# The 5x5 depthwise convolution of layer 0, taken over 16 image lines at once

## The chip, the core and the metric

The kernel runs on one core of one Trainium2 chip. A core has five engines that run beside each other and wait for one another through semaphores: TensorE (PE, matrix products), VectorE (DVE), ScalarE (ACT), GpSimd (POOL) and SyncE (SP, which here issues the transfers). The metric is the device time of one execution in microseconds (us), the median of several runs.

## The reference

Two layers run one after the other on 16 images of 128 channels and 56 x 56 pixels, in fp32. Layer 0, which the change touches, is a routed window attention:

```python
x = x + dwconv3x3(x, pos_w, pos_b)                    # per channel
y = layernorm(x) ; q, k, v = split(y @ qkv_w + qkv_b)
# 7 x 7 windows of 8 x 8 pixels; each window attends to the 4 windows
# whose mean key fits its mean query best; 4 heads of 32 channels
o = attention(q, gathered k, gathered v)
lepe = dwconv5x5(v, lepe_w, lepe_b)                   # per channel, 25 taps
x = x + (o + lepe) @ wo_w + wo_b
x = x + gelu(layernorm(x) @ mlp_w1 + mlp_b1) @ mlp_w2 + mlp_b2
```

Layer 1 (a 3x3 convolution, a small state-space recurrence over 8 tokens per pixel, a group norm) follows and is not touched.

## The kernel before

All of layer 0 is written out in one program order, and each engine keeps that order (`_chain`). Channels lie on the 128 partitions. An image is 7 blocks of 8 lines, 448 columns each (`BLK`), and a block holds 7 windows. The images go through a software pipeline: while image `im` attends, the next image `nxt` is normalised and projected, and the one after it (`far`) begins its 3x3 convolution on POOL.

**Steps.** `step(im, nxt, t)` runs once for each of the 49 windows; r = t // 7 is the window row and c = t % 7 the place in it. A step does `scores` (PE, into the PSUM tile `ps`, of which there is one), `largest` (DVE, L415), `exponentials` (ACT, L421), `inverse` (DVE reciprocal, L427), `weights` (POOL, L431), and for earlier windows the transposes (L453, L439), their copies (ACT, L459, L446) and `attend` (PE, L469). Over the seven steps of a row it also carries two layer norms and the projections: at c = 1 the sum of attention and convolution (`collect`, L516) and the output projection (L524), at c = 2 the residual (L528) and the centring product (L319), at c = 3 the square and variance product (L323, L327), at c = 4 the deviation (ACT, L331, L332), `second` (DVE, L532) and the next image's centring, at c = 5 its variance, at c = 6 its deviation and `windows` (DVE, L340, L348). POOL does the 3x3 taps of the next image (`beside`, L313, L315) spread over t = 0 to 44.

**The convolution.** `surround(im, r)` (POOL, L484) lays the 8 lines of block r with 2 lines above and below into one of three padded tiles `vpads` of 12 lines. `convolve` (DVE, L506 for the first tap, L512 for the others) multiplies one tap's shifted view by its weight and adds it to a sum in PSUM; the 25th tap writes `lepe` in SBUF. Two sums are kept in two banks (`sums_`). `convolve_on(n)` makes the next n taps of the schedule. Consecutive places in the schedule belong to two different blocks, whose sums lie in different banks:

```python
r = at // 25
r -= (r - at) % 2
convolve(images[r // NBLK], r % NBLK, (at - 25 * r) // 2)
```

A row of steps makes 4, 2, 2, 3, 3, 3, 2 taps (`TAPS`), all but one of a step's taps ahead of the reciprocal and one at the end of the step.

**MLP.** After the 49 steps, `mlp(im, nxt)` takes 7 blocks (6 for the first image) in turns m = 0, 1, ...: `expand` (PE and ACT, L542, L543), then for the block before it `contract` (PE, L548), whose last part is the DVE sum `r` (L550) and its transfer to DRAM (SP, L551). `r` comes from a pool of three buffers (`w3`). Turn m = 0 makes 10 taps, turns 1 to 5 make 7, 7, 6, 6, 6. At m = 2 SP issues the 20 gathers for the first five windows of the next image (L396), ahead of that turn's transfer of `r`. At m = 1 and 2 POOL makes 30 operations of `beside` for `far`; before that, at m = 0, it runs `surround(nxt, 2)`. In the turn before the last the scores of the next image's window 0 are begun (`open_step`), and its reciprocal follows in step 0.

Of the kernel before, what the change touches and what calls it, by code (L numbers as in the profile page):

```python
# [10 lines left out]
F32 = mybir.dt.float32  # L11
U32 = mybir.dt.uint32
AF = mybir.ActivationFunctionType
ALU = mybir.AluOpType
# [3 lines left out]
P = 128  # L18
H = W = 56
HW = H * W  # L20
WIN = 7
NW = WIN * WIN
WP = 64
BLK = 448
# [184 lines left out]
def layer0(ctx: ExitStack, tc: tile.TileContext, x, t, x1, conv):  # L209
# [42 lines left out]
    def bank(name):  # L252
        return banks.tile([P, 512], F32, tag=name, name=name)

    g0, ptt, pvt, po, *sums_ = (bank(k) for k in ("g0", "ptt", "pvt", "po", "lepe0", "lepe1"))
    ps = banks.tile([P, 2, 512], F32, tag="ps", name="ps")
# [19 lines left out]

    vpads = [cst.tile([P, 12, W + 4], F32, tag=f"vpad{k}", name=f"vpad{k}") for k in range(3)]
    for v in vpads:
# [38 lines left out]
    def centred(at, im, i):  # L317
        held["pc"] = at[:, 0:BLK]
        nc.tensor.matmul(held["pc"], lhsT=centre, rhs=im["xh"][i], start=True, stop=True)  # L319
# [155 lines left out]

    def vpad(im, r):
        return vpads[(im["b"] * NBLK + r) % 3]

    def surround(im, r):

        v = vpad(im, r)

        def put(lines, i, rows):
            nc.gpsimd.tensor_copy(  # L484
                v[:, lines, 2 : W + 2].rearrange("c r (w x) -> c w r x", x=8),
                im["kv"][:, WIN * i : WIN * i + WIN, :, 1].rearrange("c w (r x) -> c w r x", x=8)[:, :, rows, :],
            )

        put(slice(2, 10), r, slice(0, 8))
        if r == 0:  # L490
            nc.gpsimd.memset(v[:, 0:2, :], 0.0)
        else:
            put(slice(0, 2), r - 1, slice(6, 8))
        if r == NBLK - 1:
            nc.gpsimd.memset(v[:, 10:12, :], 0.0)
        else:
            put(slice(10, 12), r + 1, slice(0, 2))

    def convolve(im, r, k):

        v = vpad(im, r)
        acc = sums_[(im["b"] * NBLK + r) % 2][:, 0:BLK].rearrange("c (h w) -> c h w", w=W)
        dy, dx = divmod(k, 5)
        src = v[:, dy : dy + 8, dx : dx + W]
        if k == 0:
            nc.vector.tensor_scalar(acc, src, lep[:, 0:1], lepe_b, ALU.mult, ALU.add)  # L506
            return
        out = acc
        if k == 24:
            lepe = im["lepe", r] = w2.tile([P, BLK], F32, tag="lepe", name=f"lepe_{im['b']}_{r}")  # L510
            out = lepe.rearrange("c (h w) -> c h w", w=W)
        nc.vector.scalar_tensor_tensor(out, src, lep[:, k : k + 1], acc, ALU.mult, ALU.add)  # L512

# [31 lines left out]
    def contract(im, i, k):  # L545
        pm = (g0, po)[k % 2][:, 0:BLK]
        for s in range(3):
            nc.tensor.matmul(pm, lhsT=wm2[:, s, :], rhs=im["hid", i][:, s, :], start=(s == 0), stop=(s == 2))  # L548
        r = w3.tile([P, BLK], F32, tag="r", name=f"r_{im['b']}_{i}")
        nc.vector.scalar_tensor_tensor(r, pm, mlp_b2, im["xh"][i], ALU.add, ALU.add)  # L550
        nc.sync.dma_start(x1[im["b"]][:, i * BLK : (i + 1) * BLK], r)  # L551

    TAPS = (4, 2, 2, 3, 3, 3, 2)

    slot = [0]

    def convolve_on(count):


        for at in range(slot[0], slot[0] + count):
            r = at // 25
            r -= (r - at) % 2
            if 0 <= r < NB * NBLK:
                convolve(images[r // NBLK], r % NBLK, (at - 25 * r) // 2)
        slot[0] += count

# [4 lines left out]
    def step(im, nxt, t):  # L573
# [32 lines left out]
        if c == 6 and new:  # L606
            windows(nxt, r)
        convolve_on(TAPS[c] - 1)
        if new:
# [8 lines left out]
        inverse(im, t)  # L618
        if t in (1, 8, 17, 27):
            surround(im, 3 + (1, 8, 17, 27).index(t))  # L620
        if t in (36, 44) and new:
            surround(nxt, (t - 36) // 8)
        weights(im, t)
# [8 lines left out]
        if c % 2 == 0:  # L632
            transpose_values(im, t)
            keep_values(im, t)
        convolve_on(1)
        if waits:
# [31 lines left out]
    def mlp(im, nxt):  # L668
# [9 lines left out]
        for m in range(count + 1):  # L678
# [10 lines left out]
            if m == 0:  # L689
                transpose_weights(im, NW - 1)  # L690
                keep_weights(im, NW - 1)
                if nxt:
                    for s in (1, 2):
                        project(g0, s)
                        keep(nxt, last, s)
                convolve_on(10)
                if nxt:
                    surround(nxt, 2)
                elif early:
                    first(last, range(5, 9))  # L700
# [7 lines left out]
            if m > 0:  # L708
                contract(*blocks[m - 1], m)
            if 1 <= m <= 5:  # L710
                convolve_on((7, 7, 6, 6, 6)[m - 1])
            if far and m in (1, 2):
# [13 lines left out]
    def norm_begun(i):  # L726

        centred((g0, sums_[1])[i % 2], im, i)
        means[i] = held["pc"]
        squared(f"0_{i}")  # L730
# [8 lines left out]
    for i in range(NBLK):  # L739
# [12 lines left out]
        if i >= NBLK - 3:  # L752
            convolve_on(8)
        held["pc"] = means[i]
        windows(im, i)
        for s, at in enumerate((pvt, po, ps[:, 0, :])):
            project(at, s)
            keep(im, i, s)
# [7 lines left out]
    surround(im, 2)  # L766
    convolve_on(32)
    if NB > 1:
# [548 lines left out]
```

## Time and profile before

| what | value |
|---|---|
| median of 3 runs | 8326.0 us (8321.87 to 8326.96) |
| the profiled execution | 8321.03 us, of which the profile's span is 8319.0 us |
| layer 0 | from 0 to about 3154 us of the span |
| from one image to the next | 1406.3 to 1594.0 us at the same instruction (L382): 187.7 us |
| busy in 1500 to 2000 us | PE 463.6, DVE 457.2, POOL 410.7, ACT 363.9 of 500 us |
| one tap, 128 x 448 (L512) | 2688 in all, 677 ns each |

Times in the views are counted from the start of the span. A line of the timeline gives the start, the time from the first start to the last end, the engine, the source line, the operation, how many of it, and in brackets the idle time of the engine before it with what ended that. A line of the windows gives a stretch, its length, then the busy time of PE, PE's weight loads, DVE, ACT and POOL with the number of instructions in brackets, the granted clock of PE, the share of the DMA engines and GB/s.

### The profile page before, as it was taken

The numbers are of one execution on the slowest core, as the hardware profiler recorded it, in microseconds if no ns is written. First come the engines' busy times: TensorE is split into PE (matmuls) and PEld (weight loads), VectorE is DVE, ScalarE is ACT, GpSimd is POOL, SyncE is SP. The second block draws the span as 40 slices with busy tenths as digits, with TensorE's granted clock in tenths as the row PEclk, the third lists the DMA queues.
The fourth block names the chain that finished last, engine by engine and source line by source line (L and its number), as shares of the span: only waits on it lengthen the run. The fifth ranks groups of instructions, "written<-read, shape, count | busy, mean of one in ns | idle before, by whom it ended". The sixth has DMA issues, their size and how long they took to land.

```text
span 8319.0 us, 151598 instructions
## 1 busy us (share of the span) xinstructions
PE 7858.1 (94%) x52860; PEld 3316.4 (40%) x52860; DVE 7746.6 (93%) x10342; ACT 5659.3 (68%) x10598; POOL 7064.8 (85%) x5696
## 2 busy tenths in 40 slices
PE   5999999999999998999999999999999999999997
PEld 3444444444444453333333333333333333333332
DVE  7999999999999976999999999999999999999997
ACT  4777777777777755666666666666666666666665
POOL 7888888888888725899999989999999999999987
PEclk8999999999999998999999999999999999999998
DMA  3333333333333332334333333334334334333333
GB/s 65 86 87 88 85 89 88 87 87 87 88 86 87 79 85 80 87 89 105 98 92 99 101 92 98 96 92 104 95 93 108 86 98 108 84 101 102 89 93 80
DMA packets 764424, 757.86 MB, mean 91 GB/s; under 512 B 188688, under 2 KB 663952, under 8 KB 761616
## 3 DMA queue, kind: packets, MB, share of 16 engines
q1 hardware_dynamic: 763664, 748.18, 34.9%
q8 instruction: 422, 6.91, 0.4%
q14 instruction: 338, 2.77, 0.1%
HBM read 439.61 MB, written 102.76 MB: 65 GB/s over the span
## 4 chain that ended last, share of the span: by engine, by line
DVE 39%; POOL 25%; PE 18%; issue 10%; ACT 7%; DMA 1%; SPq 0%; POOLq 0%; ACTq 0%; DVEq 0%
DVE h L991 11%; DVE a L1001 10%; DVE h L1002 6%; POOL cst L1006 5%; POOL xh L315 5%; POOL e L431 4%; PE a L973 4%; POOL tap L313 3%; DVE lepe L512 3%; PE x L984 2%; POOL dtx L925 2%; DVE sst L415 2%; PE pq L1015 2%; DVE ud L960 2%; PE pq L184 1%
## 5 line engine op out<-in xcount | busy, mean ns | idle before, releaser
L1006 POOL TENSOR_TENSOR cst<-h,cb 128x1792 f32<-128x1792 f32 x784 | 3129.8, 3999 | 375.4 <-DVE h L1002 301.2
L976 ACT ACTIVATE a<-a 128x896 f32<-128x896 f32 x1568 | 1415.8, 903 | 1119.7 <-PE x L984 678.6
L991 DVE TENSOR_TENSOR h<-x,bb 128x896 f32<-128x896 f32 x1568 | 1696.0, 1082 | 91.0 <-PE x L984 51.2
L512 DVE SCALAR_TENSOR_TENSOR lepe<-vpad,lep,lepe 128x448 f32<-128x448 f32 x2688 | 1717.0, 677 | 0.5
L973 PE MATMUL a<-dt,adec 32*128 32x448 f32 x6272 | 1613.0, 590 | 35.6 <-DVE h L1002 16.2
L984 PE MATMUL x<-dtx,amask 32*128 32x448 f32 x6272 | 1616.1, 591 | 32.2 <-DVE h L991 24.5
L1002 DVE TENSOR_TENSOR h<-a,h 128x896 f32<-128x896 f32 x1344 | 1466.8, 1091 | 45.8
L1001 DVE TENSOR_TENSOR a<-a,h 128x896 f32<-128x896 f32 x1344 | 1463.7, 1089 | 3.7 <-ACT a L976 3.7
L431 POOL TENSOR_SCALAR e<-e,sst,zero 128x256 f32<-128x256 f32 x1568 | 861.1, 560 | 466.2 <-DVE sst L427 417.6
L421 ACT ACTIVATE e<-ps,sst 128x256 f32<-128x256 f32 x1568 | 728.6, 469 | 521.6 <-DVE sst L415 471.0
L315 POOL TENSOR_TENSOR xh<-xh,tap 128x448 f32<-128x448 f32 x749 | 859.4, 1147 | 43.7
L973 PEld LDWEIGHTS a<-dt,adec 32*128 32x128 f32 x6272 | 472.2, 184 | 1050.9 <-DVE h L1002 474.0
L184 PE MATMUL pq<-pad,conv 128*128 128x448 f32 x1890 | 834.7, 559 | 0.0
L1015 PE MATMUL pq<-cst,sel 128*32 128x448 f32 x6272 | 730.2, 550 | 1.0 <-POOL cst L1006 1.0
L415 DVE TENSOR_REDUCE sst<-ps 128x2 f32<-128x512 f32 x784 | 539.8, 688 | 107.4 <-PE ps L409 83.6
L146 ACT ACT_TABLE_LOAD x491 | 630.0, 1283 | 9.2 <-PEq L1308 0.7
L984 PEld LDWEIGHTS x<-dtx,amask 32*128 32x128 f32 x6272 | 473.1, 184 | 400.1 <-DVE h L991 378.7
L453 PE MATMUL ptt<-ident,e 128*128 128x128 f32 x3136 | 538.4, 283 | 97.0 <-POOL e L431 80.3
L409 PE MATMUL ps<-sel,q 32*64 32x256 f32 x6272 | 537.2, 411 | 51.8 <-ACT e L421 45.6
L313 POOL TENSOR_SCALAR tap<-pad,pos,zero 128x448 f32<-128x448 f32 x749 | 548.7, 733 | 35.7
L453 PEld LDWEIGHTS ptt<-ident,e 128*128 128x128 f32 x3136 | 366.6, 141 | 420.4 <-POOL e L431 240.8
L459 ACT COPY att<-ptt 128x512 f32<-128x512 f32 x784 | 458.6, 585 | 73.7 <-PE ptt L453 65.8
(173 smaller groups left out, 12025.5 us busy)
## 6 DMA issues: line engine op xcount, KB each, us to landing
sel<-kv SPq DMA_DIRECT2D x3136, 64.0 KB
bb<-db SPq DMA_DIRECT2D x336, 448.0 KB
cb<-dc SPq DMA_DIRECT2D x336, 448.0 KB
pad<-x SPq DMA_DIRECT2D x32, 784.0 KB
x<-r SPq DMA_DIRECT2D x112, 224.0 KB
pad<-x SPq DMA_DIRECT2D x16, 1568.0 KB
db<-bs SPq DMA_DIRECT2D x112, 224.0 KB
dc<-cs SPq DMA_DIRECT2D x112, 224.0 KB
```

Of the source, the lines that this page charges most:

```text
L184: self.nc.tensor.matmul(bank[:, 0:BLK], lhsT=self.weights[:, k, :], rhs=self.pad[:, 8 * i + dy : 8 * i + dy + 8, dx : dx + W], start=(k == ...
L315: nc.gpsimd.tensor_add(im["xh"][i], im["xh"][i], held["tap"])
L431: nc.gpsimd.tensor_scalar(e, e, im["st", w][:, 2, p : p + 1], zero, ALU.mult, ALU.add)
L453: nc.tensor.transpose(ptt[:, P * (2 * p + h) : P * (2 * p + h + 1)], e[:, h * P : (h + 1) * P], ident)
L512: nc.vector.scalar_tensor_tensor(out, src, lep[:, k : k + 1], acc, ALU.mult, ALU.add)
L973: nc.tensor.matmul(a[:, k, :], lhsT=adec[rows, l4, :], rhs=p["dt"][rows, h, :], start=True, stop=True)
L976: nc.scalar.activation(p["a", l, jp], p["a", l, jp], AF.Exp)
L984: nc.tensor.matmul(x[:, k, :], lhsT=mask[rows, l4, :], rhs=p["dtx"][rows, h, :], start=True, stop=True)
L991: nc.vector.tensor_mul(p["h", l][:, own(jp), :], px["x"], weight)
L1001: nc.vector.tensor_mul(a, a, before)
L1002: nc.vector.tensor_add(p["h", l][:, own(jp), :], a, p["h", l][:, own(jp), :])
L1006: nc.gpsimd.tensor_mul(c, p["h", l], p["gate", 1, l].unsqueeze(1).to_broadcast([P, 4, BLK]))
```

## The change

The tile sum covers two blocks: 16 lines, 896 columns, in one PSUM tile `acc` of two banks (1024 columns). A unit u is the pair of blocks 2u and 2u + 1; unit 3 is block 6 alone, 448 columns wide. An image has four units of 25 taps. The 25th tap of a pair is two instructions of 448 columns, one for each block's `lepe`. There is one sum and not two, so consecutive taps go to the same sum. `vpads` are two tiles of 20 lines and not three of 12; blocks that lie in one tile need no copied edge lines between them, so `surround` makes fewer copies, and it is called at other places (steps 3, 5 and 22 for the image itself, 38 and 40 for the next, turns 2 and 4 of the MLP). The taps are dealt out anew: 2, 1, 1, 2, 1, 2, 1 in the steps of rows 0 to 4, two in each of steps 35 to 46, one in step 47, none in step 48 and in turn 0, then 4, 4, 4, 4, 4, 5 in turns 1 to 6. `lepe` has three buffers and `r` two, where it was the other way round. The lead-in before the first step makes 25 taps (4, 4, 4, 13), where it made 56 places of the old schedule.

```diff
@@ -252,7 +252,8 @@
     def bank(name):
         return banks.tile([P, 512], F32, tag=name, name=name)
-    g0, ptt, pvt, po, *sums_ = (bank(k) for k in ("g0", "ptt", "pvt", "po", "lepe0", "lepe1"))
+    g0, ptt, pvt, po = (bank(k) for k in ("g0", "ptt", "pvt", "po"))
+    acc = banks.tile([P, 1024], F32, tag="lepe", name="lepe")
     ps = banks.tile([P, 2, 512], F32, tag="ps", name="ps")
@@ -274,7 +275,7 @@
     zero = cst.tile([P, 1], F32, tag="zero0", name="zero0")
     nc.vector.memset(zero, 0.0)
-    vpads = [cst.tile([P, 12, W + 4], F32, tag=f"vpad{k}", name=f"vpad{k}") for k in range(3)]
+    vpads = [cst.tile([P, 20, W + 4], F32, tag=f"vpad{k}", name=f"vpad{k}") for k in range(2)]
     for v in vpads:
         nc.gpsimd.memset(v, 0.0)
@@ -473,43 +474,47 @@
-    def vpad(im, r):
-        return vpads[(im["b"] * NBLK + r) % 3]
     def surround(im, r):
-        v = vpad(im, r)
-        def put(lines, i, rows):
+        v = vpads[r // 2 % 2]
+        def put(at, i, rows):
             nc.gpsimd.tensor_copy(
-                v[:, lines, 2 : W + 2].rearrange("c r (w x) -> c w r x", x=8),
+                v[:, at : at + rows.stop - rows.start, 2 : W + 2].rearrange("c r (w x) -> c w r x", x=8),
                 im["kv"][:, WIN * i : WIN * i + WIN, :, 1].rearrange("c w (r x) -> c w r x", x=8)[:, :, rows, :],
             )
-        put(slice(2, 10), r, slice(0, 8))
+        at = 2 + 8 * (r % 2)
+        put(at, r, slice(0, 8))
         if r == 0:
             nc.gpsimd.memset(v[:, 0:2, :], 0.0)
+        elif r % 2 == 0:
+            put(0, r - 1, slice(6, 8))
+        if r == NBLK - 1:
+            nc.gpsimd.memset(v[:, at + 8 : at + 10, :], 0.0)
+        elif r % 2:
+            put(at + 8, r + 1, slice(0, 2))
+    def convolve(im, u, k):
+        n = min(2, NBLK - 2 * u)
+        dy, dx = divmod(k, 5)
+        src = vpads[u % 2][:, dy : dy + 8 * n, dx : dx + W]
+        out = acc[:, 0 : n * BLK].rearrange("c (h w) -> c h w", w=W)
+        if k == 0:
+            nc.vector.tensor_scalar(out, src, lep[:, 0:1], lepe_b, ALU.mult, ALU.add)
+        elif k < 24:
+            nc.vector.scalar_tensor_tensor(out, src, lep[:, k : k + 1], out, ALU.mult, ALU.add)
         else:
-            put(slice(0, 2), r - 1, slice(6, 8))
-        if r == NBLK - 1:
-            nc.gpsimd.memset(v[:, 10:12, :], 0.0)
-        else:
-            put(slice(10, 12), r + 1, slice(0, 2))
-    def convolve(im, r, k):
-        v = vpad(im, r)
-        acc = sums_[(im["b"] * NBLK + r) % 2][:, 0:BLK].rearrange("c (h w) -> c h w", w=W)
-        dy, dx = divmod(k, 5)
-        src = v[:, dy : dy + 8, dx : dx + W]
-        if k == 0:
-            nc.vector.tensor_scalar(acc, src, lep[:, 0:1], lepe_b, ALU.mult, ALU.add)
-            return
-        out = acc
-        if k == 24:
-            lepe = im["lepe", r] = w2.tile([P, BLK], F32, tag="lepe", name=f"lepe_{im['b']}_{r}")
-            out = lepe.rearrange("c (h w) -> c h w", w=W)
-        nc.vector.scalar_tensor_tensor(out, src, lep[:, k : k + 1], acc, ALU.mult, ALU.add)
+            for i in range(n):
+                r, lines = 2 * u + i, slice(8 * i, 8 * i + 8)
+                lepe = im["lepe", r] = w3.tile([P, BLK], F32, tag="lepe", name=f"lepe_{im['b']}_{r}")
+                nc.vector.scalar_tensor_tensor(
+                    lepe.rearrange("c (h w) -> c h w", w=W), src[:, lines], lep[:, k : k + 1], out[:, lines],
+                    ALU.mult, ALU.add,
+                )
     def collect(im, r):
         o = held["o"] = w1.tile([P, BLK], F32, tag="o", name=f"o_{im['b']}_{r}")
@@ -546,25 +551,29 @@
         pm = (g0, po)[k % 2][:, 0:BLK]
         for s in range(3):
             nc.tensor.matmul(pm, lhsT=wm2[:, s, :], rhs=im["hid", i][:, s, :], start=(s == 0), stop=(s == 2))
-        r = w3.tile([P, BLK], F32, tag="r", name=f"r_{im['b']}_{i}")
+        r = w2.tile([P, BLK], F32, tag="r", name=f"r_{im['b']}_{i}")
         nc.vector.scalar_tensor_tensor(r, pm, mlp_b2, im["xh"][i], ALU.add, ALU.add)
         nc.sync.dma_start(x1[im["b"]][:, i * BLK : (i + 1) * BLK], r)
-    TAPS = (4, 2, 2, 3, 3, 3, 2)
-    slot = [0]
+    tapped = [0]
     def convolve_on(count):
-        for at in range(slot[0], slot[0] + count):
-            r = at // 25
-            r -= (r - at) % 2
-            if 0 <= r < NB * NBLK:
-                convolve(images[r // NBLK], r % NBLK, (at - 25 * r) // 2)
-        slot[0] += count
+        for at in range(tapped[0], tapped[0] + count):
+            if at < 100 * NB:
+                convolve(images[at // 100], at % 100 // 25, at % 25)
+        tapped[0] += count
+    def taps(t):
+        r, c = divmod(t, WIN)
+        return (2, 1, 1, 2, 1, 2, 1)[c] if r < 5 else 2 if t < 47 else 1 if t == 47 else 0
+    COPIES = {3: (0, 4), 5: (0, 5), 22: (0, 6), 38: (1, 0), 40: (1, 1)}
     def open_step(im, t):
         scores(im, t)
@@ -605,7 +614,7 @@
             second(out, row)
         if c == 6 and new:
             windows(nxt, r)
-        convolve_on(TAPS[c] - 1)
+        convolve_on(min(taps(t), 1))
         if new:
             if t == 1:
                 position(nxt, 1, (8,))
@@ -616,10 +625,8 @@
                 beside(nxt, 2 + k // count, k % count)
         exponentials(im, t)
         inverse(im, t)
-        if t in (1, 8, 17, 27):
-            surround(im, 3 + (1, 8, 17, 27).index(t))
-        if t in (36, 44) and new:
-            surround(nxt, (t - 36) // 8)
+        if t in COPIES and (nxt or not COPIES[t][0]):
+            surround((im, nxt)[COPIES[t][0]], COPIES[t][1])
         weights(im, t)
         if c == 1 and new and r:
             project(g0, 2)
@@ -632,7 +639,7 @@
         if c % 2 == 0:
             transpose_values(im, t)
             keep_values(im, t)
-        convolve_on(1)
+        convolve_on(max(taps(t) - 1, 0))
         if waits:
             piece(im, nxt, out, row, c, r)
@@ -693,10 +700,7 @@
                     for s in (1, 2):
                         project(g0, s)
                         keep(nxt, last, s)
-                convolve_on(10)
-                if nxt:
-                    surround(nxt, 2)
-                elif early:
+                if not nxt and early:
                     first(last, range(5, 9))
             if m < count:
                 expand(*blocks[m], 2)
@@ -707,8 +711,10 @@
                     gather(nxt, w)
             if m > 0:
                 contract(*blocks[m - 1], m)
-            if 1 <= m <= 5:
-                convolve_on((7, 7, 6, 6, 6)[m - 1])
+            if 1 <= m <= 6:
+                convolve_on((4, 4, 4, 4, 4, 5)[m - 1])
+            if m in (2, 4) and nxt:
+                surround(nxt, 1 + m // 2)
             if far and m in (1, 2):
                 for k in range(len(OPS)):
                     beside(far, m - 1, k)
@@ -725,7 +731,7 @@
     def norm_begun(i):
-        centred((g0, sums_[1])[i % 2], im, i)
+        centred((g0, po)[i % 2], im, i)
         means[i] = held["pc"]
         squared(f"0_{i}")
@@ -750,10 +756,10 @@
             surround(im, 0)
             surround(im, 1)
         if i >= NBLK - 3:
-            convolve_on(8)
+            convolve_on(4)
         held["pc"] = means[i]
         windows(im, i)
-        for s, at in enumerate((pvt, po, ps[:, 0, :])):
+        for s, at in enumerate((pvt, ps[:, 0, :], ps[:, 1, :])):
             project(at, s)
             keep(im, i, s)
     if NB > 1:
@@ -764,7 +770,8 @@
     for w in range(AHEAD):
         gather(im, w)
     surround(im, 2)
-    convolve_on(32)
+    surround(im, 3)
+    convolve_on(13)
     if NB > 1:
         for i in range(2):
             for k in range(len(OPS)):
```

## The prediction

> **What bounds the kernel now.** The change lies in layer 0, so I read first the windows view for one stretch of steps and one MLP of the same image, then the timeline of each engine through one row of steps (1499.55 to 1520.81 us) and through the MLP, and last the lead-in, where the same taps run with and without a partner.
>
> ```profile
> 1500.00:1522.00 22.00, 20.39 (x230) 11.09 (x229) 20.39 (x40) 17.75 (x51) 19.16 (x30) 1.00 0.31 85
> 1592.00:1625.00 33.00, 31.12 (x99) 15.29 (x97) 28.02 (x51) 14.31 (x24) 28.90 (x34) 1.00 0.28 90
> ```
>
> In the steps PE and DVE are both busy 20.39 of 22 us: neither share says which one holds the row. In the MLP PE is busy 31.1 of 33 and DVE 28.0. The row is read from the waits that end last, in the timelines of DVE and PE:
>
> ```profile
> 1505.13 0.68 DVE L528 SCALAR_TENSOR_TENSOR xh<-pvt,vec,xh 128x448 f32<-128x448 f32 x1
> 1508.67 0.69 DVE L415 TENSOR_REDUCE sst<-ps 128x2 f32<-128x512 f32 x1 [0.30 <-PE ps L409]
> 1512.43 0.62 DVE L532 TENSOR_TENSOR y<-g,rstd 128x448 f32<-128x448 f32 x1 [0.42 <-ACT rstd L332]
> ...
> 1509.12 1.02 PE L327 MATMUL pvt<-sq,mean 128*128 128x448 f32 x2 [0.22 <-ACT sq L323]
> 1513.11 1.02 PE L319 MATMUL g<-xh,centre 128*128 128x448 f32 x2 [0.32 <-DVE y L532]
> ```
>
> A row is one chain through its two layer norms. From the reduce of c = 0 at 1499.55 ACT runs without a gap through exponentials and copies to 1502.83; PE then runs L354, L453, L524 to 1505.10; the residual starts at 1505.13; PE again without a gap to the scores of c = 3; then square, L327, deviation, y at 1512.43, L319, the scores of c = 5, and in the same way through c = 6 to the reduce of the next row at 1520.81. On it DVE contributes reduces, residual and y, which start 0.02 to 0.1 us after PE or ACT lets them. The taps fill the time between. So 21.26 us for this row is what the chain takes; the other rows of this image take 21.42, 21.56, 21.64 and 21.96. Over five rows that leaves 1.5 us above the chain, some 2.2 us with the broken rows at both ends, and it is all that faster taps could take.
>
> In the MLP the sums r start 4.5 us apart or when their buffer comes free, and the last one is late through PE; this is DVE, then SP:
>
> ```profile
> 1596.48 0.68 DVE L550 SCALAR_TENSOR_TENSOR r<-po,vec,xh 128x448 f32<-128x448 f32 x1 [1.50 <-PE po L548]
> 1614.78 0.69 DVE L550 SCALAR_TENSOR_TENSOR r<-po,vec,xh 128x448 f32<-128x448 f32 x1 [0.40 <-DMA x<-r]
> 1622.09 0.68 DVE L550 SCALAR_TENSOR_TENSOR r<-po,vec,xh 128x448 f32<-128x448 f32 x1 [0.96 <-PE po L548]
> 1622.69 1.86 DVE L512 SCALAR_TENSOR_TENSOR lepe<-vpad,lep,lepe 128x448 f32<-128x448 f32 x3
> 1624.46 0.16 DVE L427 RECIPROCAL sst<-sst 128x2 f32<-128x2 f32 x1
> ...
> 1598.09 14.36 SPq L396 DMA_DIRECT2D sel<-kv  x20
> 1612.55 10.57 SPq L551 DMA_DIRECT2D x<-r  x6
> ```
>
> PE's blocks start at 1596.28, 1600.79, 1605.30: 4.51 us each, without a gap. The 20 gathers hold SP until 1612.55, so the transfer of turn 2's r starts there, and its buffer is free at 1614.78: the fifth r waits for it today, with three buffers.
>
> **Price of a tap.** From the timeline of the lead-in:
>
> ```profile
> 75.88 2.86 DVE L512 SCALAR_TENSOR_TENSOR lepe<-vpad,lep,lepe 128x448 f32<-128x448 f32 x4
> 91.48 14.28 DVE L512 SCALAR_TENSOR_TENSOR lepe<-vpad,lep,lepe 128x448 f32<-128x448 f32 x24
> ```
>
> At 75.88 four taps go to one sum, each needing the one before: (2.86 - 0.68)/3 = 0.727 us from start to start. At 91.48 the taps alternate between two sums: (14.28 - 0.68)/23 = 0.592. A wide tap is nowhere in this trace. What 448 more columns cost is bounded by two plain operations on PSUM, L516 (448 columns, 614 ns) and L991 (896, 1082 ns): 0.468. So a wide tap should take 1.06 with a stranger behind it and 1.195 with a tap of its own sum behind it. Its columns run over the edge of a bank; no row shows whether that costs, and I take nothing, with 0.1 us per wide tap in the MLP (2.4 per image) as the upper end.
>
> The Trainium skill, VectorE: DVE Perf Modes, The DRAIN you can't avoid, says that the next operation waits for the pipe to empty, with or without a semaphore. By it two old taps would cost two full durations, 1.354 us, a wide one 1.145, and 72 wide taps in 16 images would bring some 240 us as an estimate. The rows at 91.48 and 75.88 say otherwise: independent taps overlap, dependent ones do not.
>
> **The change, part by part.** Before, an image has 7 x 25 = 175 taps; after, 72 wide and 31 of 448. If all were isolated DVE would give up 175 x 0.592 - 72 x 1.06 - 31 x 0.592 = 8.9 us per image. Where it gives them up decides.
>
> *Steps 0 to 34*: 95 taps (56.2 us) become 48 wide and 4 narrow (53.2). *Steps 35 to 48*: 38 taps (22.5) become 25 narrow ones (14.8). Together 10.7 us of DVE work off, but beside the chain above. c = 0 falls from 3.03 to 2.91 and c = 4's recip comes earlier, yet the residual and y still wait for PE and ACT. Two wide taps make c = 3 and c = 5 0.3 us longer for DVE (2.92 against 2.65 and 2.61); behind c = 3 the deviation on ACT covers it, behind c = 5 y slips by 0.1, covered by PE's L439. In the steps that also hold a 3x3 tap (t = 10, 19) that cover goes and 0.25 to 0.35 us shows. I take 0.5 us per image off; bounds 2.2 off and 1.2 on.
>
> *Turn 0*: ten taps (5.9 us) go, and POOL no longer waits 5.36 us for them at `surround`. Nothing follows from it: the first r comes at 1596.48 through PE, which runs from y of step 48 through ACT's table load and copies, and POOL's chain ends at 1623.04 before the reciprocal at 1624.46 and is not what ends last. The fewer edge copies on POOL (6 x 0.29 us per image) hide in the same way.
>
> *Turns 1 to 6*, from the first r at zero. r costs 0.60 to the next start, so turns 1 to 3 take 0.60 + 3 x 1.195 + 1.06 = 5.25 on DVE against PE's 4.51: the fourth r is due at 15.7. With two buffers it now needs the transfer that the fifth r needed, free at 1614.78 - 1596.48 = 18.3. Fourth at 18.3, fifth 23.55, sixth 28.8. Turn 6 puts five taps (six instructions) where none were: 0.60 + 4 x 1.195 + 2 x 0.592 = 6.55, to 35.35; then the 3x3 tap 0.6, the reduce of window 0 0.6, the last r 0.6, step 0's wide tap 1.06: the reciprocal of window 0 at 38.2. Before it was 1624.46 - 1596.48 = 27.98. The wait is queued on DVE ahead of that reciprocal, and POOL's weights, PE's transposes and all of step 1 wait for it: 10.2 us per MLP (11 in the first image's, which has six blocks), in 15 MLPs. With taps at 1.06 throughout, the same walk gives 8.9; without the wait for r 7.6.
>
> *Clock*: PE stands idle for about 10 us there, where it stood 2.21 us. Behind such a wait in the image that ends at 2940 us L524 took 1.70 us against 1.02 elsewhere, and its steps 1 to 5 13.15 us against 12.79 in an image without: 0.4; in the first image the steps after the MLP lose 1.6. About half of the MLPs pay it already. I take 0.5 more per MLP.
>
> *Lead-in*: the first weights at 121.03 wait for POOL's 3x3 taps, not for DVE; POOL gets three more copies, 1 us.
>
> Sum: 15 x (10.2 - 0.5 + 0.5) + 1 = 154 us. The profiled execution, 8321.03 (span 8319.0 and 2 around it), becomes 8475; from the median of 8326.0 it is 8480. Below 0.2%, some 17 us, a difference could not be told from none.
>
> **A rule that goes against the change.** VectorE is idle in the MLP's last turns only through PE (0.96 us at 1622.09), so it was not what ended them. The Trainium skill, Perfetto Trace Analysis, Optimizing Scalar/DVE Operations, advises the opposite there: where VectorE isn't saturated but causes bubbles elsewhere, breaking instructions up lets work finish sooner. It gives no price.
>
> **Rivals.**
> - *The steps are bound by DVE after all* (faster). For it: DVE 93% busy there, waits on its reduces by name (ACT for L415 15.9 us in 105). If all 10.7 us came off the steps and the MLP cost 8.9, 15 x -1.8 = -27: 8299. It decides once the steps shrink by more than the MLP grows. Against it: the chain above and PE's dense rows. 0.07.
> - *Both cancel* within 17 us: the steps give 8 to 10. 0.05.
> - *No wait for r*, because the transfer lands earlier or SP's gathers do: 7.6 per MLP, 8326 + 15 x 7.6 = 8440. In the main case's range.
> - *More is lost*: 1.6 of clock, 1.2 in the steps, 2.4 at the bank edge: at 13 per image 8326 + 195 = 8521, at all of it 8559.
>
> **How the numbers follow.** The first case and its variants (slower) hold 0.88; the likeliest gives 8480. Low end: the MLP at 8.9 and half of the steps' 10.7 coming off, 15 x (8.9 - 5) = 58: 8385. High end: 8535, between the two of the last rival. Below 8385 lie most of the two cancelling cases, 0.12 together.
>
> **What would show it.** In the profile after: the wide tap about 1.145 us, 1.19 from start to start in the MLP; the fourth r of an MLP waiting for DMA x<-r, about 2.6 us; from first r to the reciprocal of window 0 about 38 us; PE waiting some 10 us for POOL's weights there; rows of steps still near 21.3 us; the instruction L382 returning after about 198 us. Rows of 20.5 us or less would make the first rival right, and an MLP of 28 us would break the forecast.

## The result, and the profile after

The changed kernel takes 8509.0 us (median of 4 runs, 8506.4 to 8511.0) against 8326.5 for the kernel before in the same series: 1.0219 times as long, 95% interval 1.0206 to 1.0232. The profiled execution has a span of 8509.2 us, 190.2 more than before.

To see where they went I cut every image at four events of DVE: the reciprocal of window 0, the reduces that begin the rows of steps, the reduce of step 48, and the first r of the MLP. Means over the second to the fifteenth image, in us:

| stretch | before | after | difference |
|---|---|---|---|
| reciprocal of window 0 to the reduce of step 7 | 19.53 | 20.32 | +0.79 |
| five rows, steps 7 to 41 | 107.90 | 109.11 | +1.21 |
| steps 42 to 48 | 18.16 | 17.94 | -0.22 |
| reduce of step 48 to the first r | 14.46 | 14.46 | 0 |
| first r to the reciprocal of window 0 | 28.07 | 38.46 | +10.39 |
| one image | 188.12 | 200.30 | +12.18 |

Fourteen images give 14 x 12.18 = 170.5. The first image gives 11.5, the stretch ahead of its reciprocal 4.45, and everything behind the last image's reciprocal, layer 1 included, 3.8: together 190.2.

The windows view for one row of steps and one MLP (columns: stretch, length, then busy us and instructions of PE, PEld, DVE, ACT, POOL, the granted clock, DMA share, GB/s):

```profile
1545.24:1567.24 22.00, 20.29 (x243) 10.90 (x233) 19.92 (x31) 17.32 (x48) 17.78 (x27) 1.00 0.29 83
1487.00:1525.50 38.50, 26.85 (x87) 13.41 (x85) 35.12 (x37) 12.27 (x21) 22.65 (x28) 0.91 0.22 73
```

In the row hardly anything has changed: VectorE has 0.5 us less to do, PE is as dense as it was. In the MLP the roles are exchanged. DVE is busy 35.1 of 38.5 us, and PE, which was dense there, 26.9. The timeline of DVE shows it turn by turn:

```profile
1487.22 0.68 DVE L555 SCALAR_TENSOR_TENSOR r<-po,vec,xh 128x448 f32<-128x448 f32 x1 [0.87 <-PE po L553]
...
1492.51 0.68 DVE L555 SCALAR_TENSOR_TENSOR r<-g,vec,xh 128x448 f32<-128x448 f32 x1
1493.11 4.72 DVE L509 SCALAR_TENSOR_TENSOR lepe<-vpad,lep,lepe 128x896 f32<-128x896 f32 x4
1497.73 0.68 DVE L555 SCALAR_TENSOR_TENSOR r<-po,vec,xh 128x448 f32<-128x448 f32 x1
...
1505.53 0.69 DVE L555 SCALAR_TENSOR_TENSOR r<-g,vec,xh 128x448 f32<-128x448 f32 x1 [2.48 <-DMA x<-r]
...
1515.99 0.68 DVE L555 SCALAR_TENSOR_TENSOR r<-g,vec,xh 128x448 f32<-128x448 f32 x1
1516.58 4.72 DVE L509 SCALAR_TENSOR_TENSOR lepe<-vpad,lep,lepe 128x896 f32<-128x896 f32 x4
1521.34 1.27 DVE L514 SCALAR_TENSOR_TENSOR lepe<-vpad,lep,lepe 128x448 f32<-128x448 f32 x2
...
1523.73 0.68 DVE L555 SCALAR_TENSOR_TENSOR r<-po,vec,xh 128x448 f32<-128x448 f32 x1
1524.32 1.21 DVE L507 TENSOR_SCALAR lepe<-vpad,lep,vec 128x896 f32<-128x896 f32 x1
1525.43 0.16 DVE L428 RECIPROCAL sst<-sst 128x2 f32<-128x2 f32 x1
```

Only two of the seven r still carry a wait: the first, for PE, and the fourth, for the transfer that has to empty its buffer. All others start when DVE's queue reaches them. Turns of four wide taps are 5.2 us long. From the first r to the reciprocal it is 38.21 us, and PE and POOL stand behind it. PE's wait ends with ACT's exponentials of window 0, which need the reduce at 1523.13, queued on DVE behind the taps and the sixth r; POOL's weighing waits longer, for the reciprocal, but of that PE has only 0.19 us to bear:

```profile
1523.13 0.68 DVE L416 TENSOR_REDUCE sst<-ps 128x2 f32<-128x512 f32 x1
1524.98 1.13 PE L410 MATMUL ps<-sel,q 32*64 32x256 f32 x8 [10.49 <-ACT e L422]
1525.69 1.09 POOL L432 TENSOR_SCALAR e<-e,sst,zero 128x256 f32<-128x256 f32 x2 [14.19 <-DVE sst L428]
1526.30 1.22 PE L454 MATMUL ptt<-ident,e 128*128 128x128 f32 x4 [0.19 <-POOL e L432]
```

### The profile page after: what moved, and what is told of

It reads as the page before. It is cut to its first block, busy times and chain, and to the rows that moved or that the text cites. A ratio compares the mean times of both kernels' runs of the same rounds, so it can differ in the third digit from the quotient of the medians.

```text
span 8509.2 us, 150302 instructions
## 1 busy us (share of the span) xinstructions
PE 7891.2 (93%) x52860; PEld 3330.3 (39%) x52860; DVE 7666.9 (90%) x9190; ACT 5657.6 (66%) x10598; POOL 7025.1 (83%) x5599
## 4 chain that ended last, share of the span: by engine, by line
DVE 35%; POOL 27%; PE 19%; issue 11%; ACT 4%; DMA 3%; SPq 1%; POOLq 0%; DVEq 0%; ACTq 0%
DVE h L998 11%; DVE a L1008 9%; POOL xh L316 6%; DVE h L1009 6%; POOL cst L1013 5%; POOL e L432 5%; PE a L980 4%; POOL tap L314 4%; PE x L991 2%; DMA pad<-x 2%; POOL dtx L932 2%; PE pq L1022 2%; DVE lepe L509 2%; DVE ud L967 2%; DVE sst L416 1%
## 5 line engine op out<-in xcount | busy, mean ns | idle before, releaser
L509 DVE SCALAR_TENSOR_TENSOR lepe<-vpad,lep,lepe 128x896 f32<-128x896 f32 (+1 forms) x1472 | 1515.6, 1030 | 10.4
L316 POOL TENSOR_TENSOR xh<-xh,tap 128x448 f32<-128x448 f32 x749 | 858.2, 1146 | 43.7
```

The costliest lines, as they stand in the source:

```text
L316: nc.gpsimd.tensor_add(im["xh"][i], im["xh"][i], held["tap"])
```

## The experiments

All times are medians; the kernel before ran beside them and took 8323 to 8324 us, some 3 us less than in the series of the result, so gains of a few us against the 8509.0 there say little by themselves. In brackets stand the ratio to the kernel before and its 95% interval. "MLP" is the time from the first r to the reciprocal of window 0, "image" the length of one image as above.

### Three buffers of r

```diff
-        r = w2.tile([P, BLK], F32, tag="r", ...)
+        r = w3.tile([P, BLK], F32, tag="r", ...)
```

> The changed kernel with one edit: r of the MLP has three buffers again. Theory (the fourth r of an MLP waits for its buffer's transfer): that wait of about 2.5 us goes, the fourth r starts 15.7 to 15.9 us behind the first, and the reciprocal of window 0 comes 35.8 instead of 38.4 us behind it; 15 x 2.6 = 39 us less than the 8509 of the changed kernel, 8470. Rival (PE or the taps alone hold the MLP, the wait only stands beside it): r's wait goes, another takes its place, 38 us to the reciprocal and 8505.

Measured: 8469.2 us (1.0174, 1.0157 to 1.0191). MLP 35.6 us in the mean. DVE's timeline, from the fourth r on:

```profile
1679.50 0.68 DVE L555 SCALAR_TENSOR_TENSOR r<-g,vec,xh 128x448 f32<-128x448 f32 x1
...
1699.40 0.15 DVE L428 RECIPROCAL sst<-sst 128x2 f32<-128x2 f32 x1
```

The first r stood at 1663.77, so the fourth comes 15.73 behind it, with no wait in brackets, and the reciprocal 35.63. The wait for the transfer was a term of the sum in its full length.

### The taps of turn 6 in turn 0

```diff
+                convolve_on(5)                      # in turn 0
-            if 1 <= m <= 6:
-                convolve_on((4, 4, 4, 4, 4, 5)[m - 1])
+            if 1 <= m <= 5:
+                convolve_on(4)
```

> The changed kernel with its five taps of turn 6 put into turn 0, r in two buffers. Theory (DVE's queue behind the last r is the path; turn 0 has about 6.8 us in which DVE waits for PE): the five taps, 4 x 1.195 + 2 x 0.592 = 5.96 us, leave the path, 32.5 us from the first r to the reciprocal of window 0, and 15 x 5.96 = 89 us less: 8420. Rival (turn 0 has no room, because route, collect and the first r stand behind the taps): the first r comes up to 5.9 us later behind the table load, the gain is lost, and the time stays near 8509.

Measured: 8424.6 us (1.0120, 1.0103 to 1.0137), MLP 32.7 us. The stretch from the reduce of step 48 to the first r is still 14.47: turn 0 took the five taps for nothing.

### Both

> Both edits: three buffers of r, and the taps of turn 6 in turn 0. Theory (both terms are on one chain and add up): about 29.9 us from the first r to the reciprocal, 15 x 8.5 = 128 less than 8509: 8381; some 55 us above the kernel before remain, of them about 29 for the turns that still hold four dependent wide taps and so 5.25 against PE's 4.51 us, the rest in steps, clock and lead-in. Rival (the clock): with PE idle for a shorter time the half-clock stretches behind the MLP go as well, some 1 us more per image, 8365. Rival (they overlap): no better than the better of the two alone.

Measured: 8383.1 us (1.0068, 1.0051 to 1.0084), MLP 29.7 us. The two gains are 39.7 and 84.4 us alone and 125.9 together (8509.0 - 8383.1), against 124.1 for their sum. They add up, as two terms of one chain do. The rival on the clock fell: PE's wait is down from 10.49 to 3.26 us, but the granted clock still reads 0.50 behind it in every image, and the stretch up to step 7 did not become shorter (20.67 us, 20.32 in the changed kernel):

```profile
1270.61 1.13 PE L410 MATMUL ps<-sel,q 32*64 32x256 f32 x8 [3.26 <-ACT e L422]
```

The clock from 1271 to 1275 us:

```profile
1271.00:1275.00 4.00, 3.81 (x18) 1.42 (x14) 4.00 (x8) 1.53 (x6) 2.94 (x5) 0.50 0.35 114
```

### Half of the taps left out in the steps

```diff
         n = min(2, NBLK - 2 * u)
+        if u in (1, 2) and k % 2:
+            return
```

> The changed kernel with every second tap of the units that are convolved in steps 0 to 34 left out (24 of 50 wide taps per image, some 25 us of VectorE's work); this part of the convolution is not computed. Theory (a row is one chain through its two layer norms, taps lie beside it): rows fall from about 21.75 to 21.0 to 21.3 us, at most 3.5 us per image, 8455 to 8480. Rival (the rows are bound by DVE): a row loses 4.8 x 1.06 = 5.1 us, rows of 16.7, 25 us per image, near 8125.

Measured: 8481.5 us (1.0191, 1.0174 to 1.0208), just above the 8480 that was the upper end of the theory. The five rows take 107.52 us instead of 109.11, an image 198.46 instead of 200.30. So 24 of 50 wide taps, 25 us of DVE's work per image, are worth 1.8 us. The rows are a chain; DVE's reduces now show what they wait for:

```profile
1559.43 0.68 DVE L416 TENSOR_REDUCE sst<-ps 128x2 f32<-128x512 f32 x1
...
1562.61 0.69 DVE L416 TENSOR_REDUCE sst<-ps 128x2 f32<-128x512 f32 x1 [1.25 <-POOL e L432]
```

So the taps hold the rows by little: the kernel before stood 0.4 us above these 107.5, the changed one 1.6.

### The copies moved to other steps

With both MLP edits:

```diff
-    COPIES = {3: (0, 4), 5: (0, 5), 22: (0, 6), 38: (1, 0), 40: (1, 1)}
+    COPIES = {1: (0, 4), 8: (0, 5), 22: (0, 6), 36: (1, 0), 43: (1, 1)}
```

> Three buffers of r and the taps of turn 6 in turn 0, as in the run with both, and beside it the copies into the padded images (surround) moved from steps 3, 5, 38, 40 to 1, 8, 36, 43. Theory (POOL copies before it weighs the step's e, and in steps c = 3 and c = 5 that weighing is on the chain; in c = 1 it is not): steps 0 to 6 fall from 20.7 to about 20.2 us, the row of steps 35 to 41 from 21.86 to 21.45, together 0.9 us per image, 14 us, 8369. Rival (the taps themselves make the steps longer, wherever POOL copies): these rows stay, 8383.

Measured: 8370.6 us (1.0053, 1.0037 to 1.0070). The total is the one expected, the parts are not. Steps up to 7 fall from 20.67 to 20.06, but the row of steps 35 to 41 goes from 21.90 to 21.82 only, and that of 7 to 13 rises from 21.85 to 22.11. In the image that I followed step by step, the step that begins at t = 9 now takes 3.30 us instead of 2.83 and that at t = 37 3.27 instead of 2.83, while that at t = 6 falls from 3.60 to 3.04. So a copy ahead of the weighing in step 5, 8 or 36 costs the step behind it 0.44 to 0.56 us, and the last two are c = 1: that c = 1 is free was wrong. It is not always paid either: the steps behind t = 22 and t = 43, also c = 1, keep their 2.83 us.

### Fewer wide taps in the MLP

With the MLP edits, the narrow taps of an image's last lines at two to four a step, and the next image's first taps behind them:

```diff
-        return (2, 1, 1, 2, 1, 2, 1)[c] if r < 5 else 2 if t < 47 else 1 if t == 47 else 0
+        if r < 5:
+            return (2, 1, 1, 2, 1, 2, 1)[c]
+        return (4, 2, 2, 3, 3, 3, 2, 4, 3, 2, 1, 1, 2, 1)[t - 35]
...
-                convolve_on(4)                      # in turns 1 to 5
+                convolve_on(3)                      # in turns 1 to 4
```

(The copies of steps 36 and 43 are here in 36 and 41, and where a step has three taps or four, all but one stand ahead of its reciprocal.)

> As the run with moved copies, but the taps are dealt so that no turn of the MLP is held by DVE: the narrow taps of an image's last lines run at two to four a step from step 35 on, eight wide taps of the next image follow in steps 43 to 48, turn 0 has five, turns 1 to 4 three each, turns 5 and 6 none. Theory (a turn with three wide taps is 0.60 + 2 x 1.195 + 1.06 = 4.05 us against PE's 4.51, so PE sets the turns as before the change): 27.4 to 28 us from first r to reciprocal against 29.75, 15 x 2 = 30 us less than 8369: 8340. Rival (steps 35 to 48 have no room): they become longer than 39.8 us by as much as the MLP gains, and the time stays near 8370.

Measured: 8356.0 us (1.0039, 1.0025 to 1.0053), between theory and rival. MLP 27.33 us, 0.7 less than in the kernel before: with three wide taps PE sets the turns again. But steps 42 to 48 rise from 17.92 to 19.69. Theory and rival were both right in part: 2.4 us gained, 1.8 given back.

### One tap less beside a 3x3 tap

```diff
-            return (2, 1, 1, 2, 1, 2, 1)[c]
+            return ((2, 1, 1, 2, 1, 2, 1), (2, 1, 1, 1, 1, 2, 1), (2, 1, 1, 2, 1, 1, 1))[r if r in (1, 2) else 0][c]
-        return (4, 2, 2, 3, 3, 3, 2, 4, 3, 2, 1, 1, 2, 1)[t - 35]
+        return (2, 3, 2, 3, 3, 3, 3, 4, 3, 2, 1, 1, 1, 1)[t - 35]
...
-            if 1 <= m <= 4:
+            if 1 <= m <= 5:
```

> As the run before it, and in the rows of steps 7 to 13 and 14 to 20 one second tap less, in the step that also holds a 3x3 tap (c = 3 and c = 5); these two taps go to step 35, and the MLP gets 20 wide taps, three in each of turns 1 to 5. Theory (behind a second wide tap and a 3x3 tap the next reduce comes late): the row of 14 to 20 falls from 22.34 to 21.3 to 21.8, that of 7 to 13 from 21.85 to 21.5, 0.7 to 1.4 us per image, 10 to 20 us, 8320 to 8330, no longer to be told from the kernel before. Rival (other waits hold these rows): they stay, 8340.

Measured: 8343.8 us (1.0022, 1.0012 to 1.0031), above the 8320 to 8330 that were expected. The row of 14 to 20 falls from 22.37 to 21.83 us and that of 7 to 13 from 22.12 to 21.78, so the taps did hold them. The MLP stays at 27.33, and the last r is once more held by PE, as in the kernel before:

```profile
1632.34 0.68 DVE L555 SCALAR_TENSOR_TENSOR r<-po,vec,xh 128x448 f32<-128x448 f32 x1 [1.14 <-PE po L553]
```

What is lost is in the row of 35 to 41 (22.69 us against 21.82 in the run before, 21.42 in the kernel before), which now begins with two wide taps of the image's lines before, and in steps 42 to 48 (18.84 against 18.16 in the kernel before).

### Two buffers of r in the kernel before

> The kernel before the change with one edit: r of the MLP has two buffers instead of three. Theory (the fourth r needs the transfer that lands 18.3 us behind the first r): the fourth r goes from 13.67 to 18.3 us, the fifth to about 22.7, the sixth to 27, and the reciprocal of window 0 from 27.98 to about 31.5 us; 15 x 3.5 = 52 us, 8376. So with the old taps the third buffer is worth more than with the new, where the fourth r is due at 15.7 anyway. Rival (PE has slack that takes it in): no change, 8324.

Measured: 8369.8 us (1.0055, 1.0038 to 1.0072), MLP 31.06 us, 3.0 more than with three buffers. DVE's timeline:

```profile
1637.20 0.68 DVE L550 SCALAR_TENSOR_TENSOR r<-g,vec,xh 128x448 f32<-128x448 f32 x1 [4.55 <-DMA x<-r]
...
1649.70 0.16 DVE L427 RECIPROCAL sst<-sst 128x2 f32<-128x2 f32 x1
```

The first r stands at 1618.89, so the fourth comes 18.31 behind it, in the place where the changed kernel has its own. This one edit, no more than a pool's name in the diff, costs 46 us by itself.

### The copies behind the weighing, before and after the change

```diff
+        weights(im, t)
         if t in COPIES and (nxt or not COPIES[t][0]):
             surround((im, nxt)[COPIES[t][0]], COPIES[t][1])
-        weights(im, t)
```

In the kernel before:

> The kernel before the change with one edit: in a step, POOL's copies into the padded images (surround) are queued behind the weighing of e instead of ahead of it. Theory (a copy ahead of the weighing makes PE's transposes of the weights late, and the next reduce with them: in the trace of before, the step behind a copy is longer by 0.36 at t = 9, 0.55 at 18, 0.58 at 28, 0.28 at 37 and 0.4 at 45, together 2.2 us per image): these steps fall to the 2.83, 3.56, 3.04, 2.83 and 2.58 to 2.65 us of their kind, 16 x 2 = 32 us less than 8324: 8292, faster than both kernels. Rival (POOL's queue is full there, a copy behind the weighing only delays the next step's weighing): the same time, 8324.

In the changed kernel:

> The changed kernel with the same one edit, the copies queued behind the weighing. Theory: of the steps' cost of the change the part that is POOL's copies goes, 0.54 at t = 6 and 0.4 at t = 39, about 1 us per image, 15 us: 8494; the rows of steps 7 to 13 and 14 to 20, which hold no copy here, stay at 21.84 and 22.33. Rival (the taps make these steps longer): 8509.

Measured: the kernel before becomes slower, 8337.2 us (1.0017, 1.0008 to 1.0027); the changed one goes to 8498.1 (1.0210, 1.0193 to 1.0227), 10.9 less. The interval overlaps that of the changed kernel (1.0206 to 1.0232), so the steps have to decide: the one at t = 6 falls from 3.59 to 3.05 us, the one at t = 39 from 4.00 to 3.55. POOL and PE around t = 38 of the changed kernel as it was:

```profile
1643.78 0.59 POOL L484 COPY vpad<-kv 128x448 f32<-128x448 f32 x1
1644.31 0.20 POOL L492 MEMSET vpad<- 128x120 f32 x1
1644.49 1.09 POOL L432 TENSOR_SCALAR e<-e,sst,zero 128x256 f32<-128x256 f32 x2
...
1645.10 0.97 PE L454 MATMUL ptt<-ident,e 128*128 128x128 f32 x4 [0.64 <-POOL e L432]
```

PE's transposes wait for the weighing, which stands behind a copy, and PE's centring and the next scores stand behind the transposes. With the order exchanged:

```profile
1630.80 1.09 POOL L432 TENSOR_SCALAR e<-e,sst,zero 128x256 f32<-128x256 f32 x2
1631.84 0.61 POOL L484 COPY vpad<-kv 128x448 f32<-128x448 f32 x1
1632.39 0.20 POOL L492 MEMSET vpad<- 128x120 f32 x1
...
1631.41 0.97 PE L454 MATMUL ptt<-ident,e 128*128 128x128 f32 x4
```

The wait is gone, and the row falls from 21.87 to 21.42 us, the steps ahead of 7 from 20.32 to 19.72. In the kernel before the delay was only moved: the step at t = 18 falls from 4.11 to 3.55 us and the one at 19 rises from 3.05 to 3.62, and the step at 28 rises from 3.62 to 4.51. In the same way steps 9 and 37 give 0.36 and 0.28 us to steps 10 and 39, which rise by 0.37 and 0.46. The rival holds there: what comes later on POOL pays instead, and this exchange does not make the copies free in the kernel before.

### The last deal, with the copies behind

```diff
-        return (2, 3, 2, 3, 3, 3, 3, 4, 3, 2, 1, 1, 1, 1)[t - 35]
+        return (2, 3, 2, 3, 3, 3, 3, 3, 2, 3, 1, 1, 1, 1)[t - 35]
...
-                convolve_on(5)                      # in turn 0
+                convolve_on(6)
```

> The last deal of wide taps, with the copies behind the weighing, the narrow taps spread more evenly over steps 36 to 44, six wide taps in turn 0 and 15 in turns 1 to 5. Theory (copies and a full VectorE in steps 35 to 48 are what that deal still loses): the row of 7 to 13 falls from 21.77 to 21.3, that of 35 to 41 from 22.69 to about 21.7, steps 42 to 48 from 18.82 to about 18.1; 2 us per image, 8344 - 32 = 8312, at or below the kernel before. Rival (POOL's queue is full): no change, 8344.

Measured: 8336.6 us (1.0016, 1.0006 to 1.0025). Steps 42 to 48 fall to 17.92 us, but the row of 7 to 13 stays at 21.79, that of 35 to 41 rises from 22.69 to 22.91 and the steps ahead of 7 from 19.42 to 19.79: 7 us of the 32 that were expected. This is the best deal of wide taps that I found, and it is still not faster than the kernel before.

### Every wide tap as two narrow ones

```diff
-        elif k < 24:
-            nc.vector.scalar_tensor_tensor(out, src, lep[:, k : k + 1], out, ...)
+        if k < 24:
+            for i in range(n):
+                s, o = src[:, 8 * i : 8 * i + 8], out[:, 8 * i : 8 * i + 8]
...
+                    nc.vector.scalar_tensor_tensor(o, s, lep[:, k : k + 1], o, ...)
```

> The changed kernel with every wide tap issued as two of 448 columns, at the same place; everything else as changed. Theory (a wide tap that waits for the one before it, 1.19 us, is worth no more than two independent narrow ones, 2 x 0.592 = 1.184, and the MLP's length comes from how many taps stand in a turn, not from their form): r to reciprocal within 0.5 us of 38.4; the steps 0.12 us longer per wide tap where VectorE holds them, 0.5 to 2.5 us per image; 8517 to 8545. Rival (the wide form itself, over the edge of a bank, is what costs): the split taps are faster, below 8495.

Measured: 8672.6 us (1.0418, 1.0400 to 1.0435). Neither theory had this. One turn of its MLP:

```profile
1774.83 5.75 DVE L512 SCALAR_TENSOR_TENSOR lepe<-vpad,lep,lepe 128x448 f32<-128x448 f32 x8
1780.49 0.68 DVE L558 SCALAR_TENSOR_TENSOR r<-po,vec,xh 128x448 f32<-128x448 f32 x1
```

Eight narrow taps start (5.75 - 0.68)/7 = 0.724 us apart. That is the price of taps that depend on one another, though neighbours here write different halves of the sum. The 0.592 of the kernel before came with two sums in two tiles, not merely with different columns. So a pair of taps costs 1.184 us as two narrow ones in two tiles, 1.19 as one wide tap behind a wide one, and 1.45 as two narrow ones in one tile. It is the wide form that makes one common tile bearable; against what was there before it saves nothing in the MLP. By the semaphore records of the trace each of these taps starts 25 ns behind the signal of the tap just before it, as the wide taps do behind theirs, where in the kernel before a tap starts 100 ns ahead of its neighbour's signal. That looks like a wait for the neighbour, which the arithmetic does not need: the order kept for a tile, then. It is not shown, since no run took the wait out.

## Why the prediction was right, and where its steps were off

**The MLP: right, term by term.** The walk gave 38.2 us from first r to reciprocal; the MLP shown takes 38.21, all of them 38.46 in the mean. The fourth r came at 18.31 with a wait of 2.48 (18.3 and 2.6). Removing single terms moved the time by what they were priced at: 39.7 for the wait of r (39 forecast in the expectation), 84.4 for the taps of turn 6 (89), and with three wide taps to a turn PE sets the turns again. So the cause is shown: 25 wide taps, the last of them as two narrow ones, in six turns are 30 us of DVE, where the turns had held 32 taps of 0.592, 19 us, and turn 0, which had room for ten narrow taps and has room for five wide ones, was left empty. One sign was read wrongly: PE's 10 us end with ACT's exponentials, so with the reduce of window 0, and not with POOL's weights behind the reciprocal. Both stand in the same queue on DVE, so the sum did not suffer from it.

**The steps: the term that was mis-sized.** I took 0.5 us per image off. The parts are +0.5 ahead of step 7, taken between the shortest of the fourteen stretches (19.30 and 19.81 us), because the clock lengthens the others, and by medians +0.89 in the five rows and -0.22 in steps 42 to 48: 1.17 us more, at my upper bound of 1.2. The idea held, that a row is a chain and the taps lie beside it (half of them away: 1.8 us of 25). Two prices did not. Behind the 3x3 taps I had 0.25 to 0.35 us each. Against the rows without a 3x3 tap, steps 10 and 11 are 0.56 longer together where they were even before, and steps 19 and 20 are 1.03 longer, against 0.15 before. DVE's timeline of the second case, and POOL beside the 3x3 tap:

```profile
1582.44 0.69 DVE L416 TENSOR_REDUCE sst<-ps 128x2 f32<-128x512 f32 x1 [0.69 <-POOL e L432]
1583.05 1.15 DVE L509 SCALAR_TENSOR_TENSOR lepe<-vpad,lep,lepe 128x896 f32<-128x896 f32 x1
1584.10 1.24 DVE L304 SCALAR_TENSOR_TENSOR xh<-pad,pos,xh 128x448 f32<-128x448 f32 x1
1585.26 0.15 DVE L428 RECIPROCAL sst<-sst 128x2 f32<-128x2 f32 x1
1585.34 1.13 DVE L509 SCALAR_TENSOR_TENSOR lepe<-vpad,lep,lepe 128x896 f32<-128x896 f32 x1
1586.38 0.68 DVE L416 TENSOR_REDUCE sst<-ps 128x2 f32<-128x512 f32 x1
...
1583.72 1.14 POOL L316 TENSOR_TENSOR xh<-xh,tap 128x448 f32<-128x448 f32 x1
```

The queue is full from reduce to reduce: 3.94 us, nothing waits. The 3x3 tap alone takes 1.24 us, where the kernel before and the run with half of the taps have 0.68, and at t = 10 it takes 1.04 where it took 0.68. The trace shows when that happens: of its 147 such taps the 43 beside which POOL ran nothing took 0.68 us each, and the 26 with POOL's addition of two SBUF tiles (L316) beside them for over 0.6 us took 1.23 to 1.44; in the kernel before it is 26 taps at 0.68 and 26 at 1.33 to 1.45. So the new order also moved these taps beside POOL's additions, a term that the prediction did not have. It is 0.36 us at t = 10 and 0.56 at t = 19; if all of it is on the path, 0.2 and 0.3 us remain, about what I had. No run moved these taps away again by itself. And I gave POOL's copies no price where they went, in steps 3, 5 and 38. By the run with the copies behind the weighing they cost 0.54 us at t = 6 and 0.45 at t = 39 of each image; the whole 0.5 ahead of step 7 goes with them (in that run its shortest stretch is 19.26 us).

**The clock: right in kind, its size in part by luck.** PE stands idle 10.49 us, and the clock behind it is this, in the changed kernel and then in the deal with one tap less, where PE waits there for 1.54 us at most in fourteen of fifteen MLPs:

```profile
1524.00:1528.00 4.00, 2.83 (x13) 1.41 (x14) 4.00 (x6) 2.00 (x8) 2.23 (x4) 0.50 0.32 106
```

```profile
1624.00:1636.00 12.00, 10.36 (x45) 5.06 (x45) 10.15 (x15) 4.79 (x9) 9.10 (x12) 1.00 0.33 120
```

In the steps up to 7 the mean is 0.51 us above the shortest; in the kernel before it is 0.22 above the median, which lies beside the shortest there. That makes 0.3 us per image behind the MLP, where I had 0.5. Another 0.3 lies in the rows, whose mean is 0.37 above the median (0.04 before), and there I had nothing: in three of the fourteen images the clock fell to 0.50 for some 3 us in steps 20 and 21, 63 us behind the reciprocal, and the five rows took 110.2 to 110.5 us instead of 108.7. One of them:

```profile
986.00:989.00 3.00, 3.00 (x26) 1.22 (x26) 2.10 (x4) 1.50 (x5) 1.92 (x4) 0.50 0.30 87
```

Ahead of it PE waits no longer than in the images where the clock stays at 1.00, so what set it off is open. The total, 0.6 us, came near to mine through a term that I did not have.

**The lead-in: not decided.** I had 1 us, the profiled execution 4.45. But the nine other profiles with the same lead-in have their first reciprocal anywhere from 110.5 to 116.4 us, and the three with the old one at 112.3 to 113.1. So this part of the profiled difference is not to be put down to the change. The 3.8 us behind the last image stay open: they lie in the main in layer 1, whose code is the same and whose recurrence takes 5068.5 to 5081.5 us over all profiles, but in all eleven profiles with the wide layout this end is longer (5381.3 to 5391.1 us) than in the three with the old one (5377.5 to 5378.6).

**The sum.** 36 us of span were missing from the forecast: 25 from the steps (15 x 1.67), 3.4 from the lead-in, 3.8 at the end, the rest MLP and clock. The wide tap was 1.145 us long and 1.19 from start to start, as worked out, so the edge of the bank costs nothing that these rows show; it was not tried by itself. The Trainium skill, VectorE: DVE Perf Modes, The DRAIN you can't avoid, from which the prediction worked out 240 us, also points to operations that start earlier because nothing holds them; the prediction left that out, and the rows it set against the rule, 0.592 us from start to start at 0.68 us each, go that way. The rival in which DVE bounds the steps is refuted by the run with half of the taps; "no wait for r" by 1505.53.

**The rule.** The Trainium skill, Perfetto Trace Analysis, Optimizing Scalar/DVE Operations, advises to break instructions up where VectorE causes bubbles without being saturated. The changed kernel has such a bubble, PE's 10.49 us, but VectorE is busy 35.1 of the 38.5 us around it, so the advice's condition hardly holds there. The same taps in smaller pieces, in one tile, made the kernel 163.6 us slower: what helped was fewer taps in the turn, not smaller ones.

## What to carry to other kernels

Price an instruction from start to start in the place where it will stand, behind its own kind and in its tile, not by its isolated saving: a coarser form that ends the alternation of two sums may cost as much as the pair it replaces. Work given back by one engine is worth what the chain there can take, here 1.8 of 25 us, and work put into a stretch that another engine had just filled costs all that exceeds that engine's turn. Look in a diff for the smallest edits: a pool with one buffer fewer cost 46 us in the kernel before and 40 in the changed one, where it is about a fifth of the loss.

## What the runs showed of the hardware that I had not expected

Taps that write disjoint halves of one PSUM tile start 0.724 us apart, 25 ns behind the neighbour's signal, as dependent ones do; in two tiles it was 0.592. After PE had been idle for 10 us its granted clock read 0.50, and it still did for some 3 us after the first new product (1524.98 to about 1528.4), in which a group of eight score products took 1.13 instead of 0.68 us. It was so behind shorter waits too: the clock read 0.50 behind all fifteen MLPs of the run with both edits, where PE mostly waited 3.26 us, and behind seven of fifteen in the kernel before, at mostly 2.2 us. A 3x3 tap on DVE, which reads two SBUF tiles, took 0.68 us with POOL idle and up to 1.45 beside POOL's additions. A copy of 0.8 us on POOL, an engine that is busy 83% of the span, cost the step behind it up to 0.56 us where it stood ahead of the weighing that PE waits for, and at t = 3, 22 and 40 of the changed kernel nothing.
